# Two gated banded layers on one core: the right projection in four 64x64 tiles instead of two 64x128 tiles with an exchanged second copy

## The chip, the cores and the metric

One NeuronCore of a Trainium2 chip runs the whole program. The metric is the device time of one execution in microseconds, the median of three runs. The engines named below are PE (TensorE, matrix products), PEld (its weight loads), ACT (ScalarE), DVE (VectorE), POOL (GpSimd) and SP (SyncE, which issues most DMAs).

## The reference

Input and output are one 512 x 512 image with 64 channels, float32. Two layers run in sequence, each as x + layer(group_norm(x)). A layer is, with D = 64 and H = 128:

```python
xn = _ln(x, norm_scale, norm_bias)
left = (xn @ Wl + bl) * mask * jax.nn.sigmoid(xn @ Wlg + blg)
right = (xn @ Wr + br) * mask * jax.nn.sigmoid(xn @ Wrg + brg)
out_gate = jax.nn.sigmoid(xn @ Wog + bog)
out = _banded_ingoing(left, right, WIN)
out = _ln(out, out_norm_scale, out_norm_bias) * out_gate
return out @ Wo + bo
```

`_banded_ingoing` mixes along the row axis: row i of the result is the sum, over the nine rows k from i - 4 to i + 4, of left at (k, i) times right at row k, for every column j and every channel on its own. All weights act on 64 or 128 channels, and everything is float32.

## The kernel before

**Tiling.** The 512 rows are cut into nine overlapping blocks of 64 rows, of which 56 (60 at the borders) give output. The two halves of the 512 columns are processed together: partitions 0 to 63 hold the 64 rows of a block at columns j, partitions 64 to 127 the same rows at columns 256 + j. A unit is 8 columns of each half (`JU`), a chunk 8 units; a layer has 36 chunks, and a period of the schedule handles one chunk. So there are 288 units a layer and 576 in all.

**Stages of a unit**, each a step with a name. `load` (SP) fetches the tile z; `scale`, `move` (POOL, some on DVE), `inner` (DVE statistics), `centre`, `resc` (POOL) normalise it. `ztr` transposes it on PE into a bank of PSUM (line 569), `keep0` copies this on ACT into the ring `ZT` (line 583) and `keep1` copies it on ACT a second time, with the two row halves exchanged, into `zT` (line 589). `proj0` and `proj1` are the two halves (4 columns each) of the right projection on PE (`crossed`, line 610): the products with `Wr` and `Wrg` side by side. `sig` is the sigmoid of the gate on ACT (line 630), `right` the product on DVE into `RO` (line 634).

**Stages of a chunk's mixing.** `band` on PE multiplies, per channel, the banded left matrix `A` with `RO` in 64x64 tiles of the array (line 711), `copy` on ACT writes the result back into `RO`. Then, 16 units later, `ost` (statistics), `sa`, `sd` (the norm's factors), `norm0` to `norm7` (ACT, or POOL where the word carries a "!"), `turn0`, `turn1` (transposes on PE, line 844), `gate` (the output gate on PE from `ZT`, line 826), `gated` (its sigmoid on ACT), `tg` (DVE), `last` (the product with `Wo` on PE, line 883), `end` (the residual on DVE), `stp` (the store). Layer 1 also has `sums` on PE (statistics for layer 2's group norm, line 904), layer 2 has `seed` on PE (the bias, line 876).

**Why halves are exchanged.** The band's product of a channel takes row half e of the partitions and writes row half e or its exchange, by the channel's slab s (`e ^ s`, line 723). So for half of the channels (s = 1) `RO` has to hold the two column halves exchanged. `crossed` gets this by taking `ZT` for s = 0 and the exchanged copy `zT` for s = 1 as the stationary operand.

**What sets the order.** Two tables, `FIRST` (line 39) and `SECOND` (line 69), list the steps of a period for layers 1 and 2. A word such as `proj0:2@0` means: half 0 of the projection of the unit 2 places behind the period's first, into PSUM bank pair 0. The loop at line 1117 runs through the table once a period, and each engine executes its instructions in that order. Three bank pairs (`take`, `give`, lines 224 to 235) are shared by `ztr`, `proj`, `gate`, `turn` and `band`; a pair is given back by the step that has read it, for `ztr` this is `keep1`.

The steps of PE in the order of the two tables, each read as a ring, are:

```
FIRST   proj0 proj1 ztr last sums gate band band turn1 turn0 gate proj1 band last turn0 turn1 proj0
        band gate ztr sums last band sums ztr turn1 turn0 proj0 band band gate proj0 turn1 turn0 band
        last ztr gate proj1 last sums turn1 turn0 gate proj1 proj0 ztr sums last turn1 turn0 proj1
        proj0 proj1 ztr sums last sums gate gate turn0 turn1 proj1 proj0 ztr sums last ztr turn0 turn1
        proj0 proj1
SECOND  seed turn1 ztr turn0 last proj0 proj1 band ztr band seed gate proj0 turn0 turn1 band last gate
        turn1 turn0 seed band proj1 ztr last gate proj0 seed ztr turn0 turn1 last proj0 proj1 gate
        proj1 ztr seed turn0 turn1 last ztr proj0 proj1 seed ztr last gate turn0 turn1 proj1 seed
        proj0 proj1 proj0 gate last band turn1 turn0 gate band seed turn0 last ztr turn1 band proj0
        band gate proj1
```

In the profile nearly all instructions carry line 492, that of the helper which keeps the program's order, so they are told apart by the names of their tiles: `banks<-pack,ZT` and `banks<-pack,zT` are the projection, `banks<-RO,A` the band, `banks<-ident,z` and `banks<-ident,on` the transposes `ztr` and `turn`, `banks<-ZT,pack` the gate, `bank<-pack,ZH` is `last`, `acc<-XR` is `sums`, `bank<-pieces,ones` is `seed`. A float32 product on PE makes two records, a transpose one.

Of the kernel before, what the change touches and what calls it, by code (L numbers as in the profile page):

```python
# [31 lines left out]
RING = LAG + 2  # L32
# [8 lines left out]
last:-1 sig1:-1 move:4 sums:-3 scale:10 right0:-1 stp:-2 norm7:0 load:11 keep0:0 ost2:6 gate:0@0  # L41
keep1:0 inner:9 gated:0 right1:-1 band:3@1 norm2:0! norm3:0! move:6 scale:11 move:10 band:2@2
ost3:7 copy:3 turn1:0@0 turn0:0@1 gate:1@1 copy:2 norm0:1 gated:1 inner:7 proj1:0@2 end:-1 norm3:1
tg:0 sig1:0 band:7@0 ost0:4 norm5:1! inner:4 norm1:1! norm7:1 norm4:1! norm6:1! inner:10 norm2:1
last:0 fetch:1 end:0 turn0:1@1 move:11 copy:7 turn1:1@1 proj0:0@0 right1:0 tg:1 norm3:2 sig0:0
resc:2 resc:1 norm4:2 band:0@2 ost1:4 norm1:2 copy:0 right0:0 norm5:2! gate:2@1 ztr:1@0 scale:8
gated:2 norm6:2! sums:-2 last:1 keep0:1 keep1:1 fetch:2 ost0:7 ost2:5 norm2:2! stp:0 inner:6
norm7:2! band:1@2 sums:0 ztr:2@0 copy:1 ost0:5 keep0:2 turn1:2@1 ost1:6 inner:11 norm0:2! load:12
turn0:2@0 inner:5 proj0:1@2 move:8 keep1:2 sa:4 inner:8 norm0:3 scale:12 centre:9 tg:2 sig0:1
band:4@0 sd0:4 norm1:3 end:1 norm3:3! band:6@1 load:13 norm6:3 norm2:3! norm7:3! right0:1 sd1:4  # L50
# [3 lines left out]
norm3:4! ost2:12 norm1:4! sig1:1 last:3 scale:13 norm4:4 scale:14 sums:-1 ost2:15 ost1:13  # L54
turn1:4@2 centre:5 keep1:3 ost3:8 ost3:11 turn0:4@2 gate:5@1 resc:4 gated:5 ost2:10 ost0:11 resc:6
ost1:11 right1:1 tg:4 proj1:2@0 norm5:5! norm7:5! norm4:5! proj0:3@2 ost2:8 ost1:10 norm6:5
ztr:4@1 norm2:5! sig1:2 sig0:3 norm1:5! end:3 centre:8 keep0:4 right1:2 resc:5 right0:3 sums:3
fetch:4 norm3:5 norm0:5 keep1:4 last:4 centre:7 ost3:12 turn1:5@2 load:15 ost0:10 turn0:5@1 end:4
norm6:6 norm7:6! norm1:6 proj1:3@0 centre:10 tg:5 sig1:3 proj0:4@1 sig0:4 stp:-1 proj1:4@2 ost3:10
right1:3 norm4:6! ost1:8 ztr:5@0 norm5:6! sig1:4 fetch:5 right0:4 norm0:6 sums:1 ost0:8 keep0:5  # L60
ost3:9 last:5 sums:2 right1:4 load:16 gate:6@1 resc:7 keep1:5 ost1:9 ost0:9 gate:7@2 ost3:14 sa:8
ost3:13 turn0:6@0 norm2:6! norm3:6! gated:6 gated:7 norm0:7 ost0:14 sd0:8 scale:15 stp:1 fetch:7
move:15 turn1:6@0 sd1:8 norm4:7! norm1:7! centre:11 tg:6 fetch:6 end:5 proj1:5@1 proj0:5@2 sig1:5
ztr:6@0 norm7:7! norm5:7! norm6:7 load:17 sig0:5 norm2:7 right1:5 sums:4 keep0:6 last:6 norm3:7!
move:13 right0:5 ztr:7@2 keep1:6 keep0:7 keep1:7 turn0:7@0 turn1:7@1 sd2:8 proj0:6@1 proj1:6@2
tg:7 stp:3 stp:2 end:6 scale:17 norm5:8! resc:8 load:18 norm4:8 sig0:6 stp:4 fetch:8 sig1:6
# [3 lines left out]
seed:0 inner:8 turn1:1@2 inner:5 ztr:1@0 right1:0 move:11 ost3:5 stp:-1 keep0:1 turn0:1@2 norm5:2!  # L70
last:0 keep1:1 norm0:2 tg:1 inner:10 norm2:2 resc:2 centre:4 norm6:2! proj0:1@1 sa:4 sig0:1
proj1:1@0 norm7:2 end:0 sig1:1 right0:1 band:4@2 copy:4 ztr:2@1 right1:1 band:5@0 centre:5
centre:6 keep0:2 keep1:2 stp:0 sd0:4 norm3:2 seed:1 gate:2@2 inner:11 copy:5! fetch:2 norm4:2
# [4 lines left out]
ost2:9 last:2 ost0:13 ost1:9 fetch:3 end:2 ost3:9 stp:2 keep0:3 sig1:2 right1:2 keep1:3 gate:4@1  # L78
resc:6 proj0:3@2 norm7:4! load:15 seed:3 ost1:15 norm5:4 ztr:4@0 gated:4 centre:10 ost0:9
turn0:4@1 centre:9 sig0:3 ost1:13 load:16 ost0:15 turn1:4@0 right0:3 last:3 keep0:4 keep1:4  # L80
# [4 lines left out]
ost1:10 keep1:5 scale:14 keep0:6 proj0:5@1 move:12 keep1:6 proj1:5@0 ost2:11 norm5:6! fetch:6  # L85
sig0:5 seed:5 stp:3 ztr:7@2 right0:5 fetch:5 last:5 norm7:6 ost2:8 ost2:10 norm2:6! sig1:5
gate:6@1 right1:5 keep0:7 norm6:6! norm0:6 ost2:13 ost0:8 keep1:7 turn0:6@0 scale:15 norm3:6
turn1:6@2 proj1:6@2 fetch:9 gated:6 ost2:12 norm0:7! ost1:8 load:19 sa:8 sig1:6 norm5:7! end:5
# [4 lines left out]
ost1:12 seed:7 resc:8 turn0:8@2 copy:9 last:7 ztr:8@1 gated:8 norm3:8! resc:9 turn1:8@0 norm0:9!  # L93
inner:14 stp:5 ost3:12 norm1:9! inner:12 keep0:8 scale:18 band:14@0 keep1:8 ost2:14 norm5:9 stp:6
tg:8 proj0:8@1 stp:4 ost3:15 norm6:9! norm4:9! ost0:12 band:10@2 norm3:9! fetch:8 fetch:12 norm7:9
# [63 lines left out]
def tile_two_banded_layers(  # L159
# [51 lines left out]
    turns = cycle(range(3))  # L211
# [271 lines left out]
    w = views(pack)  # L483
# [99 lines left out]
    def kept(u: Unit):  # L583
        en.scalar.activation(
            ZT[:, u.at % RING].rearrange("c k (n p) -> c n k p", n=2),
            u.pt.rearrange("c n (k p) -> c n k p", p=S), AF.Identity, bias=1.0,
        )

    def kept_again(u: Unit):
        u.t = ztp.tile([P, JU // 2, P], F32, tag=f"zT{u.at % 2}", name="zT")  # L590
        en.scalar.activation(
            u.t.rearrange("c k (n p) -> c n k p", n=2),
            u.pt.rearrange("c n (k p) -> c n k p", p=S)[:, ::-1], AF.Identity, bias=1.0,
        )
        give(u.bank)
# [14 lines left out]
    def crossed(u: Unit, q: int, w: bass.AP, b: str):  # L610

        u.banks[q], pr = take(b)
        pr = pr.rearrange("p (e k h) -> p e k h", e=2, k=JQ // 2)
        turns = ZT[:, u.at % RING], u.t
        for k in range(JQ // 2):
            for s in range(2):
                for e in range(2):
                    part = slice(e * D, (e + 1) * D)
                    en.tensor.matmul(
                        pr[:, e, k, :].rearrange("p (g s x) -> p g s x", g=2, s=2)[:, :, s],  # L620
                        lhsT=turns[s][part, q // 2 + k],
                        rhs=w[part].rearrange("c (g s x) -> c g s x", g=2, s=2)[:, :, s],
                        start=True, stop=True,
                    )
        return pr
# [290 lines left out]
    def layer(src: bass.AP, dst: bass.AP, w: dict, stats: bool, then=None):  # L916
        per = LH // JC
        n_chunks = len(blocks) * per
        units, outs, lefts, posts = {}, {}, {}, {}
        for c in range(n_chunks):  # L920
            b = blocks[c // per]
            for k in range(NU):
                t = c * NU + k
# [5 lines left out]
        for n in range(n_left):  # L929
            t = n - n_left - 1  # L930
# [77 lines left out]
        def on_keep(n, t, alt, b):  # L1008
            if t in units:
                (kept_again if n else kept)(units[t])  # L1010

# [215 lines left out]
    ZT = keep.tile([P, RING, JU // 2, P], F32, name="ZT")  # L1227
# [19 lines left out]

    ztp = ctx.enter_context(tc.tile_pool(name="ztp", bufs=1))
    wk = ctx.enter_context(tc.tile_pool(name="wk", bufs=3))
# [40 lines left out]
```

## Time and profile before

| | us |
|---|---|
| median of three runs | 4331.73 |
| lowest and highest run | 4329.06, 4340.09 |
| span of the profiled execution, first to last instruction | 4342.3 |

The profiled execution is one of its own; its span is all that the profile has of its time, and it is 10.6 us longer than the median. Layer 1's first transposes start at 229.6 us, behind the statistics of the input and the weights; the last products of layer 2's left operand start at 2358.3 us. The stretch from 600 to 2120 us lies in the midst of layer 1, that from 2700 to 4150 us in the midst of layer 2.

How to read it: a row of groups gives engine, operation, output and inputs, shapes and count, then busy time in us and the mean of one in ns. In PE's rows "64*128" and the like are the rows and columns of the array that the instruction takes, the shape behind it is that of the moving operand. A row of the time order gives start, length from the first start to the last end, and the count of records; ends of PE's records are modelled, so the distance from one row's start to the next row's start tells what a step takes.

### The profile page before, as it was taken

The page shows a single profiled execution, that of the slowest core. Times are in us where ns is not written, and L with a number is a line of the kernel's source. Part 1 is how long each engine was busy: PE and PEld are TensorE (multiplying, and loading weights), DVE is VectorE, ACT ScalarE, POOL GpSimd, SP SyncE. Part 2 cuts the span into 40 slices and gives each one's busy share as a digit, 9 for nine tenths or more (in the row PEclk, how much of TensorE's full clock was granted, in tenths as well). Part 3 has the DMA queues.
Part 4 walks back from the last instruction along what each step waited for, and adds up shares of the span by engine and source line. Part 5 has one row for each costly group of instructions (what it writes and reads, how often), then busy time and mean ns, then how long its engine had stood idle before and what let it go on. Part 6 is the DMA issues. An engine that isn't in the chain of part 4 may idle for free.

```text
span 4342.3 us, 223298 instructions
## 1 busy us (share of the span) xinstructions
PE 3778.1 (87%) x94986; PEld 3263.8 (75%) x94986; DVE 3667.7 (84%) x9911; ACT 3189.2 (73%) x5976; POOL 3754.3 (86%) x4962
## 2 busy tenths in 40 slices
PE   0169899999898999999995889898989899989998
PEld 0058787878787878888874778787878787878786
DVE  8988787878787888888877788898989898989897
ACT  0048787878787877777773778787878787878787
POOL 2379898989898999999956789898989898989894
PEclk9989999999999999999997999999999999999999
DMA  9844545454545454445434344445454545454533
GB/s 393 313 110 108 134 113 143 115 141 114 140 115 138 112 141 120 131 123 129 125 109 114 101 136 124 139 128 138 123 142 122 143 120 145 121 145 121 152 112 100
DMA packets 695719, 596.26 MB, mean 137 GB/s; under 512 B 138310, under 2 KB 549990, under 8 KB 692420
## 3 DMA queue, kind: packets, MB, share of 16 engines
q1 hardware_dynamic: 692212, 580.43, 47.1%
q8 instruction: 748, 12.26, 1.2%
q14 instruction: 247, 2.02, 0.2%
q0 software_dynamic: 2512, 1.56, 0.1%
HBM read 436.71 MB, written 149.74 MB: 135 GB/s over the span
## 4 chain that ended last, share of the span: by engine, by line
PE 46%; POOL 20%; DVE 11%; DMA 9%; SPq 7%; issue 6%; ACT 2%; POOLq 0%; DVEq 0%; ACTq 0%
PE banks L492 35%; POOL z L492 13%; PE bank L492 8%; SPq L492 7%; POOL on L492 6%; PE acc L492 2%; DVE RO L492 2%; DMA z<-in_x_dram 2%; DMA z<-mid_x 2%; DVE gn_st L492 2%; DVE sti L492 1%; DVE sto L492 1%; DVE XR L492 1%; DVE ZH L492 1%; DMA raw<-in_L_conv_Wl_dram 1%
## 5 line engine op out<-in xcount | busy, mean ns | idle before, releaser
L492 POOL TENSOR_SCALAR on<-RO,rs,nm 128x128 f32<-128x128 f32 x2520 | 1129.1, 464 | 157.1 <-PE banks L492 111.2
L492 ACT ACTIVATE on<-RO,nm,rs 128x128 f32<-128x128 f32 x2088 | 971.2, 499 | 106.6 <-PE banks L492 95.2
L492 PE MATMUL banks<-pack,ZT 64*128 64x128 f32 x9216 | 992.3, 287 | 24.1 <-DVE RO L492 13.7
L492 PE MATMUL banks<-pack,zT 64*128 64x128 f32 x9216 | 953.1, 279 | 1.8 <-ACT zT L492 1.0
L492 POOL TENSOR_TENSOR z<-z,ga 128x512 f32<-128x512 f32 x556 | 716.8, 1296 | 261.0 <-DMA z<-mid_x 117.7
L492 ACT ACTIVATE sg<-banks 128x512 f32<-128x512 f32 x1170 | 696.6, 596 | 296.7 <-PE banks L492 270.9
L492 PEld LDWEIGHTS banks<-pack,ZT 64*128 64x128 f32 x9216 | 781.9, 194 | 148.4 <-DVE RO L492 47.5
L492 DVE TENSOR_TENSOR RO<-banks,sg 128x512 f32<-128x512 f32 x1152 | 777.3, 682 | 113.3 <-ACT sg L492 76.6
L492 DVE BATCH_NORM_STATS2 sto<-RO 128x6 f32<-128x256 f32 x2304 | 847.0, 413 | 5.2 <-ACT RO L492 4.0
L492 DVE SCALAR_TENSOR_TENSOR ZH<-banks,pack,ZH 128x896 f32<-128x896 f32 (+1 forms) x576 | 668.0, 1160 | 186.3 <-PE banks L492 155.4
L492 PEld LDWEIGHTS banks<-pack,zT 64*128 64x128 f32 x9216 | 762.2, 194 | 3.5 <-ACT zT L492 2.3
L492 PEld LDWEIGHTS banks<-RO,A 64*64 64x64 f32 x36864 | 617.7, 136 | 159.8 <-DVE RO L492 50.8
L492 PE MATMUL banks<-RO,A 64*64 64x64 f32 x36864 | 694.2, 223 | 48.6 <-issue 20.2
L492 POOL TENSOR_TENSOR z<-z,gb 128x512 f32<-128x512 f32 x556 | 715.7, 1293 | 3.3
L492 ACT COPY RO<-banks 128x1024 f32<-128x1024 f32 x540 | 539.8, 1008 | 194.5 <-PE banks L492 186.4
L492 PE MATMUL bank<-pack,ZH 128*64 128x64 f32 x18432 | 666.2, 226 | 15.7 <-DVE XR L492 5.6
L492 PEld LDWEIGHTS bank<-pack,ZH 128*64 128x64 f32 x18432 | 593.0, 139 | 76.7 <-issue 34.3
L492 ACT ACTIVATE ZH<-banks 128x896 f32<-128x896 f32 (+1 forms) x576 | 531.8, 930 | 142.6 <-PE banks L492 135.2
L492 POOL TENSOR_TENSOR z<-z,rs 128x512 f32<-128x512 f32 x586 | 614.9, 1059 | 19.7 <-DVE rs L492 19.4
L492 POOL TENSOR_TENSOR z<-z,sti 128x512 f32<-128x512 f32 x586 | 620.1, 1072 | 7.6 <-DVE sti L492 7.5
L492 DVE BATCH_NORM_STATS2 sti<-z 128x6 f32<-128x128 f32 x2344 | 505.6, 282 | 120.2 <-POOL z L492 118.0
L492 PE MATMUL banks<-ZT,pack 64*128 64x448 f32 (+1 forms) x2304 | 589.7, 584 | 9.8 <-DVE RO L492 5.5
(202 smaller groups left out, 4169.3 us busy)
## 6 DMA issues: line engine op xcount, KB each, us to landing
z<-in_x_dram SPq DMA_DIRECT2D x576, 128.0 KB
A<-left_of SPq DMA_DIRECT2D x576, 128.0 KB
z<-mid_x SPq DMA_DIRECT2D x576, 128.0 KB
gn_x<-in_x_dram SPq DMA_DIRECT2D x16, 4096.0 KB
XR<-in_x_dram SPq DMA_DIRECT2D x448, 112.0 KB
mid_x<-XR SPq DMA_DIRECT2D x448, 112.0 KB
XR<-mid_x SPq DMA_DIRECT2D x448, 112.0 KB
out_dram<-XR SPq DMA_DIRECT2D x448, 112.0 KB
```

The source lines that it names most:

```text
L492: return lambda *a, **k: tc.keep_in_program_order(f(*a, **k))
```

## The change

The second copy `kept_again` and its steps `keep1` are removed, with the tile pool of `zT`; `kept` gives the bank back. `crossed` takes `ZT` alone. It splits the 128 stationary columns, the two row halves n of a column pair, into two products of 64 columns each, and writes the result of half n to the PSUM partitions of half `n ^ s`. Each product thus takes one of four 64x64 tiles of the array, given by the channel half e (rows) and `n ^ s` (columns). There are 16 products for a half of the projection in place of 8, each with the same 128 moving columns. The tables lose the words `keep1` and are otherwise the same.

```diff
-keep1:0 inner:9 gated:0 right1:-1 band:3@1 norm2:0! norm3:0! move:6 scale:11 move:10 band:2@2
+ inner:9 gated:0 right1:-1 band:3@1 norm2:0! norm3:0! move:6 scale:11 move:10 band:2@2
...
             ZT[:, u.at % RING].rearrange("c k (n p) -> c n k p", n=2),
             u.pt.rearrange("c n (k p) -> c n k p", p=S), AF.Identity, bias=1.0,
         )
-
-    def kept_again(u: Unit):
-        u.t = ztp.tile([P, JU // 2, P], F32, tag=f"zT{u.at % 2}", name="zT")
-        en.scalar.activation(
-            u.t.rearrange("c k (n p) -> c n k p", n=2),
-            u.pt.rearrange("c n (k p) -> c n k p", p=S)[:, ::-1], AF.Identity, bias=1.0,
-        )
         give(u.bank)
...
-        turns = ZT[:, u.at % RING], u.t
+        z = ZT[:, u.at % RING].rearrange("c k (n p) -> c k n p", n=2)
         for k in range(JQ // 2):
             for s in range(2):
-                for e in range(2):
-                    part = slice(e * D, (e + 1) * D)
-                    en.tensor.matmul(
-                        pr[:, e, k, :].rearrange("p (g s x) -> p g s x", g=2, s=2)[:, :, s],
-                        lhsT=turns[s][part, q // 2 + k],
-                        rhs=w[part].rearrange("c (g s x) -> c g s x", g=2, s=2)[:, :, s],
-                        start=True, stop=True,
-                    )
+                for n in range(2):
+                    for e in range(2):
+                        part = slice(e * D, (e + 1) * D)
+                        to = slice((n ^ s) * S, ((n ^ s) + 1) * S)
+                        en.tensor.matmul(
+                            pr[to, e, k, :].rearrange("p (g s x) -> p g s x", g=2, s=2)[:, :, s],
+                            lhsT=z[part, q // 2 + k, n],
+                            rhs=w[part].rearrange("c (g s x) -> c g s x", g=2, s=2)[:, :, s],
+                            start=True, stop=True,
+                        )
         return pr
...
-                (kept_again if n else kept)(units[t])
+                kept(units[t])
...
-    ztp = ctx.enter_context(tc.tile_pool(name="ztp", bufs=1))
```

More of the change, by code (lines that the diff above doesn't have):

```diff
@@ L46 @@
 resc:2 resc:1 norm4:2 band:0@2 ost1:4 norm1:2 copy:0 right0:0 norm5:2! gate:2@1 ztr:1@0 scale:8
-gated:2 norm6:2! sums:-2 last:1 keep0:1 keep1:1 fetch:2 ost0:7 ost2:5 norm2:2! stp:0 inner:6
+gated:2 norm6:2! sums:-2 last:1 keep0:1 fetch:2 ost0:7 ost2:5 norm2:2! stp:0 inner:6
 norm7:2! band:1@2 sums:0 ztr:2@0 copy:1 ost0:5 keep0:2 turn1:2@1 ost1:6 inner:11 norm0:2! load:12
-turn0:2@0 inner:5 proj0:1@2 move:8 keep1:2 sa:4 inner:8 norm0:3 scale:12 centre:9 tg:2 sig0:1
+turn0:2@0 inner:5 proj0:1@2 move:8 sa:4 inner:8 norm0:3 scale:12 centre:9 tg:2 sig0:1
 band:4@0 sd0:4 norm1:3 end:1 norm3:3! band:6@1 load:13 norm6:3 norm2:3! norm7:3! right0:1 sd1:4
@@ L54 @@
 norm3:4! ost2:12 norm1:4! sig1:1 last:3 scale:13 norm4:4 scale:14 sums:-1 ost2:15 ost1:13
-turn1:4@2 centre:5 keep1:3 ost3:8 ost3:11 turn0:4@2 gate:5@1 resc:4 gated:5 ost2:10 ost0:11 resc:6
+turn1:4@2 centre:5 ost3:8 ost3:11 turn0:4@2 gate:5@1 resc:4 gated:5 ost2:10 ost0:11 resc:6
 ost1:11 right1:1 tg:4 proj1:2@0 norm5:5! norm7:5! norm4:5! proj0:3@2 ost2:8 ost1:10 norm6:5
 ztr:4@1 norm2:5! sig1:2 sig0:3 norm1:5! end:3 centre:8 keep0:4 right1:2 resc:5 right0:3 sums:3
-fetch:4 norm3:5 norm0:5 keep1:4 last:4 centre:7 ost3:12 turn1:5@2 load:15 ost0:10 turn0:5@1 end:4
+fetch:4 norm3:5 norm0:5 last:4 centre:7 ost3:12 turn1:5@2 load:15 ost0:10 turn0:5@1 end:4
 norm6:6 norm7:6! norm1:6 proj1:3@0 centre:10 tg:5 sig1:3 proj0:4@1 sig0:4 stp:-1 proj1:4@2 ost3:10
 right1:3 norm4:6! ost1:8 ztr:5@0 norm5:6! sig1:4 fetch:5 right0:4 norm0:6 sums:1 ost0:8 keep0:5
-ost3:9 last:5 sums:2 right1:4 load:16 gate:6@1 resc:7 keep1:5 ost1:9 ost0:9 gate:7@2 ost3:14 sa:8
+ost3:9 last:5 sums:2 right1:4 load:16 gate:6@1 resc:7 ost1:9 ost0:9 gate:7@2 ost3:14 sa:8
 ost3:13 turn0:6@0 norm2:6! norm3:6! gated:6 gated:7 norm0:7 ost0:14 sd0:8 scale:15 stp:1 fetch:7
@@ L64 @@
 ztr:6@0 norm7:7! norm5:7! norm6:7 load:17 sig0:5 norm2:7 right1:5 sums:4 keep0:6 last:6 norm3:7!
-move:13 right0:5 ztr:7@2 keep1:6 keep0:7 keep1:7 turn0:7@0 turn1:7@1 sd2:8 proj0:6@1 proj1:6@2
+move:13 right0:5 ztr:7@2 keep0:7 turn0:7@0 turn1:7@1 sd2:8 proj0:6@1 proj1:6@2
 tg:7 stp:3 stp:2 end:6 scale:17 norm5:8! resc:8 load:18 norm4:8 sig0:6 stp:4 fetch:8 sig1:6
@@ L70 @@
 seed:0 inner:8 turn1:1@2 inner:5 ztr:1@0 right1:0 move:11 ost3:5 stp:-1 keep0:1 turn0:1@2 norm5:2!
-last:0 keep1:1 norm0:2 tg:1 inner:10 norm2:2 resc:2 centre:4 norm6:2! proj0:1@1 sa:4 sig0:1
+last:0 norm0:2 tg:1 inner:10 norm2:2 resc:2 centre:4 norm6:2! proj0:1@1 sa:4 sig0:1
 proj1:1@0 norm7:2 end:0 sig1:1 right0:1 band:4@2 copy:4 ztr:2@1 right1:1 band:5@0 centre:5
-centre:6 keep0:2 keep1:2 stp:0 sd0:4 norm3:2 seed:1 gate:2@2 inner:11 copy:5! fetch:2 norm4:2
+centre:6 keep0:2 stp:0 sd0:4 norm3:2 seed:1 gate:2@2 inner:11 copy:5! fetch:2 norm4:2
 norm1:2! gated:2 centre:3 proj0:2@1 turn0:2@0 turn1:2@2 band:7@2 norm0:3! norm7:3 sd1:4 last:1
@@ L77 @@
 norm1:4! seed:2 band:3@1 norm3:4 norm0:4! copy:3 resc:7 inner:9 proj1:2@0 norm4:4 ost3:8 ztr:3@2
-ost2:9 last:2 ost0:13 ost1:9 fetch:3 end:2 ost3:9 stp:2 keep0:3 sig1:2 right1:2 keep1:3 gate:4@1
+ost2:9 last:2 ost0:13 ost1:9 fetch:3 end:2 ost3:9 stp:2 keep0:3 sig1:2 right1:2 gate:4@1
 resc:6 proj0:3@2 norm7:4! load:15 seed:3 ost1:15 norm5:4 ztr:4@0 gated:4 centre:10 ost0:9
-turn0:4@1 centre:9 sig0:3 ost1:13 load:16 ost0:15 turn1:4@0 right0:3 last:3 keep0:4 keep1:4
+turn0:4@1 centre:9 sig0:3 ost1:13 load:16 ost0:15 turn1:4@0 right0:3 last:3 keep0:4
 norm4:5 tg:4 norm3:5 centre:8 norm1:5! norm6:5 norm7:5! resc:5 load:12 proj0:4@2 ost0:14 sig0:4
@@ L84 @@
 scale:13 ost0:10 right1:4 keep0:5 scale:16 ost3:11 ztr:6@2 scale:12 norm4:6 tg:5 norm1:6! end:4
-ost1:10 keep1:5 scale:14 keep0:6 proj0:5@1 move:12 keep1:6 proj1:5@0 ost2:11 norm5:6! fetch:6
+ost1:10 scale:14 keep0:6 proj0:5@1 move:12 proj1:5@0 ost2:11 norm5:6! fetch:6
 sig0:5 seed:5 stp:3 ztr:7@2 right0:5 fetch:5 last:5 norm7:6 ost2:8 ost2:10 norm2:6! sig1:5
-gate:6@1 right1:5 keep0:7 norm6:6! norm0:6 ost2:13 ost0:8 keep1:7 turn0:6@0 scale:15 norm3:6
+gate:6@1 right1:5 keep0:7 norm6:6! norm0:6 ost2:13 ost0:8 turn0:6@0 scale:15 norm3:6
 turn1:6@2 proj1:6@2 fetch:9 gated:6 ost2:12 norm0:7! ost1:8 load:19 sa:8 sig1:6 norm5:7! end:5
@@ L93 @@
 ost1:12 seed:7 resc:8 turn0:8@2 copy:9 last:7 ztr:8@1 gated:8 norm3:8! resc:9 turn1:8@0 norm0:9!
-inner:14 stp:5 ost3:12 norm1:9! inner:12 keep0:8 scale:18 band:14@0 keep1:8 ost2:14 norm5:9 stp:6
+inner:14 stp:5 ost3:12 norm1:9! inner:12 keep0:8 scale:18 band:14@0 ost2:14 norm5:9 stp:6
 tg:8 proj0:8@1 stp:4 ost3:15 norm6:9! norm4:9! ost0:12 band:10@2 norm3:9! fetch:8 fetch:12 norm7:9
```

## The prediction

> **What bounds the kernel now.** I read the page's busy line and its chain first, then busy time by stretch, then the chain and the waits inside a steady stretch of each layer.
>
> ```profile
> span 4342.3 us, 223298 instructions
> PE 3778.1 (87%) x94986; PEld 3263.8 (75%) x94986; DVE 3667.7 (84%) x9911; ACT 3189.2 (73%) x5976; POOL 3754.3 (86%) x4962
> PE 46%; POOL 20%; DVE 11%; DMA 9%; SPq 7%; issue 6%; ACT 2%; POOLq 0%; DVEq 0%; ACTq 0%
> 600.00:2120.00 1520.00, 1416.28 (x37166) 1240.70 (x37164) 1250.29 (x3349) 1171.98 (x2162) 1421.81 (x1890) 0.98 0.49 128
> 2700.00:4150.00 1450.00, 1354.94 (x33894) 1168.85 (x33892) 1267.09 (x3373) 1198.98 (x2294) 1351.49 (x1727) 0.97 0.48 133
> by line: PE banks L492 42.3%; POOL z L492 12.0%; PE bank L492 9.3%; issue 5.9%; POOL on L492 5.5%; PE acc L492 4.7%; DMA z<-in_x_dram 4.6%; SPq L492 4.3%; DVE RO L492 1.9%; DMA mid_x<-XR 1.3%; DVE sti L492 1.3%; DVE ZH L492 1.2%; DVE XR L49
> by line: PE banks L492 31.1%; POOL z L492 17.6%; SPq L492 10.5%; POOL on L492 9.7%; PE bank L492 7.6%; issue 7.2%; DMA z<-mid_x 4.1%; DVE RO L492 2.4%; DMA out_dram<-XR 1.7%; DVE sto L492 1.3%; DVE XR L492 1.2%; DVE sti L492 1.0%; DVE rsqrt
> ```
>
> The stretch rows give length, then busy time of PE, PEld, DVE, ACT and POOL. In layer 1 (600 to 2120 us) PE and POOL are both busy for 93% and ACT for 77%; in layer 2 (2700 to 4150 us) 93%, 93% and 83%. The two chain lines are for the same stretches: PE's three names make 42.3 + 9.3 + 4.7 = 56.3% of the chain in layer 1 and 31.1 + 7.6 = 38.7% in layer 2, POOL and DMA most of the rest. ACT holds 2% of the whole chain. So of PE's busy time, 56.3 / 93.2 = 0.60 lies on the path in layer 1 and 38.7 / 93.4 = 0.41 in layer 2. **The change takes work from ACT, which hardly sets the end, and rearranges PE, which does.**
>
> The waits of PE in the two stretches say the same (who waited for whom, us, times, longest); the last two rows, of ACT's groups, are what the change removes and what it keeps:
>
> ```profile
> PE banks L492 <- POOL on L492: 33.9, 27, 4.6
> PE banks L492 <- POOL z L492: 31.7, 12, 4.0
> ...
> PE banks L492 <- POOL on L492: 70.9, 34, 5.3
> ...
> PE banks L492 <- ACT on L492: 0.4, 2, 0.2
> ...
> L492 ACT ACTIVATE zT<-banks 128x512 f32<-128x512 f32 x576 | 344.0, 597 | 0.0
> L492 ACT ACTIVATE ZT<-banks 128x512 f32<-128x512 f32 x576 | 342.4, 595 | 110.8 <-PE banks L492 107.2
> ```
>
> **ACT's part.** Removed: 576 zT copies of 597 ns, 344.0 us of busy time. PE waits 0.4 us for ACT in layer 2's stretch and ACT is 2% of the chain, so what lies under these copies is ACT's own slack. If the 2% (87 us) shrank as zT's share of ACT's work (344.0 / 3189.2 = 11%), the gain were 9 us; the least is nothing. I take -5. The bank of the transposes is also given back one copy earlier, and the projection no longer waits for the second copy; by the wait rows neither is short.
>
> **PE's part: the streams.** A half of the projection was 16 records in 64x128 tiles (two tiles at once), and becomes 32 records in 64x64 tiles (four at once), of the same 128 columns. The engine's order of time in two stretches (start, length, count) has all rows that are needed:
>
> ```profile
> 1006.81 2.15 PE L492 MATMUL banks<-RO,A 64*64 64x64 f32 x128
> 1008.89 0.71 PE L492 MATMUL banks<-ident,on 64*128 64x64 f32 x16
> 1009.44 0.97 PE L492 MATMUL banks<-ZT,pack 64*128 64x448 f32 x4
> ...
> 1021.07 0.66 PE L492 MATMUL banks<-ident,on 64*128 64x64 f32 x16
> 1021.57 0.44 PE L492 MATMUL banks<-pack,ZT 64*128 64x128 f32 x4
> 1021.85 0.39 PE L492 MATMUL banks<-pack,zT 64*128 64x128 f32 x4
> ...
> 3127.72 0.92 PE L492 MATMUL banks<-ZT,pack 64*128 64x448 f32 x4
> 3128.47 0.46 PE L492 MATMUL banks<-pack,ZT 64*128 64x128 f32 x4
> ...
> 3150.83 1.19 PE L492 MATMUL banks<-RO,A 64*64 64x64 f32 x64
> 3151.95 0.49 PE L492 MATMUL banks<-pack,ZT 64*128 64x128 f32 x4
> 3152.27 0.39 PE L492 MATMUL banks<-pack,zT 64*128 64x128 f32 x4
> 3152.50 0.39 PE L492 MATMUL banks<-pack,ZT 64*128 64x128 f32 x4
> 3152.72 0.39 PE L492 MATMUL banks<-pack,zT 64*128 64x128 f32 x4
> 3153.04 1.19 PE L492 MATMUL banks<-RO,A 64*64 64x64 f32 x64
> 3154.16 1.02 PE L492 MATMUL banks<-ZT,pack 64*128 64x448 f32 x4
> 3155.02 0.39 PE L492 MATMUL banks<-pack,ZT 64*128 64x128 f32 x4
> ```
>
> Four projection records start every 0.223 us, two at a time, so a wave of two takes 111.6 ns and a half 8 waves, 0.893 us. The band's product already runs in four 64x64 tiles: 128 records take 2.08 us to the next start (1006.81 to 1008.89), 64 take 1.12 (3150.83 to 3151.95), so 64 records are 0.96 us, a wave of four with 64 columns 60 ns. For four tiles with 128 columns the bounds are 111.6 (no dearer than two tiles) and twice 60, 120 ns. I take 113.3, the old wave plus a few ns for the two further tiles, nearer the row with the same columns. Eight waves cost 0.906 us: 0.0136 more a half, 0.22 us in a period of 16 halves. Twice the instructions do the same work in the same time.
>
> **PE's part: the switches.** The 64x128 projection stood among transposes and gates that also use 64x128 tiles. From its last start at 3152.72 to the band's first it is 0.32 us where the rhythm is 0.22: leaving 64x128 tiles costs 0.10. A band run of 64 records takes 1.12 where the streams take 0.96: first weights and leaving together 0.16. The first four projection records behind the band take 0.32 (3151.95 to 3152.27), again 0.10 for first weights of 128 columns. Sixteen transposes take 0.55 behind the band (1008.89) and 0.50 without a switch (1021.07): 0.05. A gate takes 0.86 behind the band (3154.16) and 0.75 behind the projection (3127.72): 0.11. I give 64-column weights 0.05, half of 128's, which leaves 0.11 for leaving 64x64 tiles. So a switch costs **0.15 us into the new projection, 0.16 out of it to transposes, 0.22 out of it to a gate**. A projection behind transposes pays 0.06 already (1021.57 to 1021.85 is 0.28).
>
> Now the order of the steps (the lists of PE's steps, read as rings). FIRST has 4 gate to projection (+0.60), 5 turn to projection (0.09 each, +0.45), 4 projection to ztr and 1 to turn (+0.80), 3 projection to band (no switch any more, 0.15 each, -0.45), 1 projection to last (+0.01): **+1.41 us a period**. SECOND has 4 gate to projection (+0.60), 3 projection to turn or ztr (+0.48), 4 projection to seed (0.16 as for transposes, +0.64), 2 projection to gate (+0.44), one each from ztr, turn and seed (+0.33), 2 projection to band (-0.30), 2 band to projection (0.21 each, -0.42), 2 last to projection (0.05 each, -0.10): **+1.67 us**. With the streams 1.63 and 1.89 us; 36 periods each, 59 + 68 = 127 us more of PE.
>
> The Trainium skill, TensorEngine Tiling (Array Packing), section Key Properties, says that a change of the tiling mode, not just of the tile, drains the engine. By the 0.32 against 0.22 us the trace agrees; the page gives no figure. If only the streams counted, the sum were 0.22 us a period, 16 us of PE.
>
> **On the path.** If the path stays where it is, it grows by 0.60 x 59 + 0.41 x 68 = 63 us, and a longer path of the same links can't end earlier. If PE sets everything, it is 127. PE now waits 1520 - 1416 = 104 us in 28.8 periods of 52.7 us (the chain of that stretch repeats in that time), 3.6 a period, and 2.0 would be left; POOL is as busy. I take the lower end and a third of the rest: 63 + 21 = 84.
>
> ```profile
> 1025.52 3.53 PE banks L492 x100
> ...
> 1078.22 3.53 PE banks L492 x100
> ...
> L492 PE MATMUL banks<-RO,A 64*64 64x64 f32 x36864 | 694.2, 223 | 48.6 <-issue 20.2 <-DVE RO L492 16.2 <-DVE rsqrt_u L492 8.7
> L492 PEld LDWEIGHTS banks<-RO,A 64*64 64x64 f32 x36864 | 617.7, 136 | 159.8 <-DVE RO L492 50.8 <-issue 29.6 <-ACT RO L492 26.2
> ```
>
> The band's records wait 20.2 us for "issue", that is for nothing that the profile shows, most likely for instructions: they use theirs up fastest. 18,432 further pairs on 94,986 are 19% more; I add 6 us (from 0 to twice the 20.2). Sum: 84 + 6 - 5 = **+85 us** on the profiled 4342.3, so 4427; that execution lies 10.6 above the median of 4331.73, and I predict **4417 us**. Prices of 0.15 us read from rows rounded to 0.01 are good to 7%, 9 us of the 127. So the case's own range is 4377 (63 - 9 for ACT at its most - 9) to 4474 (127 + 6 + 9).
>
> **Rivals.**
>
> 1. *A tile waits for its weights.* The new order uses tiles as AABB CCDD CCDD AABB, (row half, column half) of (0,0), (1,0), (0,1), (1,1), where a record pair is one product. The next A has to be loaded past two C and two D that wait. If the engine can't, each of four alternations a half shows a first weight load, 0.05 us: 0.20 x 1152 = 230 us on PE, half of it on the path, 4417 + 115 = 4532 (4450 to 4600). For it: the band goes round its tiles evenly, and nothing in this trace has two pairs in a row. Against it: in the band too, records of one tile follow each other in pairs and four tiles still run at once.
>
> 2. *PE's waits swallow it.* The 3.6 us of waits a period exceed the 1.63; if they are free on the path, the time stays at 4332, or at 4340 with half of the streams' 16 us on the path (4320 to 4372, where at most a third of the switches counts). Against it: more than half of layer 1's chain is PE itself.
>
> 3. *Faster: ACT's queue was the hidden limit.* Each zT delays the sigmoid, norm or copy behind it by about 0.5 us (3151.06 to 3151.54 below), DVE's products wait for sigmoids, and banks come free with them. DVE waits 76.6 us for ACT's sg in all; if half of that lies on the path and the switches fall into PE's waits, 4332 - 38 + 8 = 4302. It decides if more of ACT's delays than of PE's switches reach the path; 2% against 46% of the chain speak against it.
>
> ```profile
> 3151.06 0.59 ACT L492 ACTIVATE zT<-banks 128x512 f32<-128x512 f32 x1
> 3151.54 0.89 ACT L492 ACTIVATE on<-RO,nm,rs 128x128 f32<-128x128 f32 x2
> ...
> L492 DVE TENSOR_TENSOR RO<-banks,sg 128x512 f32<-128x512 f32 x1152 | 777.3, 682 | 113.3 <-ACT sg L492 76.6
> ```
>
> 4. *Weights never load beside a product of the same rows.* Then each of 8 waves a half would show its whole load, 136 ns by the band's weight row: 1.09 us x 1152, less PE's waits, some 5400 us. The band's 60 ns waves with loads of 136 ns refute it. The Trainium skill, TensorE: Matmul & The Clock Gate, section The mechanism, says that loads overlap only with products of another row group; here the trace says otherwise, and the trace decides.
>
> That the change doesn't do what it says is not likely: the band shows that the four tiles run at once.
>
> **Numbers.** Chances: my forecast 0.70; rival 1 0.12; rival 2 0.12 (of it 0.07 within 0.3%, 0.05 slower); rival 3 0.05; rival 4 0.01. Slower by over 0.3% (13 us, about what a measurement of this kernel can tell from no change): 0.70 + 0.12 + 0.05 + 0.01 = 0.88; within 0.07; faster 0.05. The range takes in the forecast's own, the lower half of rival 1's (where the bound of 120 ns for a wave lies too) and the top of rival 2's: 4355 to 4520.
>
> **What would show it.** Right: ACT's busy time falls by some 340 us with no end moved; a half of the projection takes about 0.91 us from first to last start in an even rhythm; 0.15 us stands between a gate or transposes and the projection, and nothing between it and the band; PE's share of the chain rises and its waits for POOL shrink. Wrong: gaps of 0.05 us inside a half (rival 1), a PE that waits for POOL as long as before (rival 2), or sigmoids that come earlier with DVE's products behind them (rival 3). A first start of the projection behind a gate in the plain rhythm would take the switches out of the sum.

## The result and the profile after

| | before, us | changed, us |
|---|---|---|
| median (lowest to highest) | 4331.73 (4328.07 to 4346.16), 5 runs | 4438.66 (4417.79 to 4440.58), 5 runs |
| span of the profiled execution | 4342.3 | 4415.6 |

The ratio is 1.0228, with a 95% interval of 1.0207 to 1.0250: 107 us slower. Forecast were 4417 us and 85 us more, in a range of 4355 to 4520. The profiled execution of the changed kernel is its fastest of five, and its span is only 73 us longer than that of the kernel before, so its trace shows the loss at its smallest.

The page after: span, busy times with instructions, PE's instruction queue (packets, MB, share), the chain by engine, and PE's groups of the projection and of the band.

```profile
span 4415.6 us, 259199 instructions
PE 3839.3 (87%) x113418; PEld 3175.8 (72%) x113418; DVE 3683.1 (83%) x9911; ACT 2938.3 (67%) x5400; POOL 3748.7 (85%) x4962
q8 instruction: 891, 14.60, 1.4%
PE 61%; DVE 11%; POOL 9%; DMA 7%; SPq 6%; issue 5%; ACT 2%; DVEq 0%; POOLq 0%; ACTq 0%
L492 PE MATMUL banks<-pack,ZT 64*64 64x128 f32 x36864 | 1221.1, 278 | 38.1 <-DVE RO L492 18.7
L492 PE MATMUL banks<-RO,A 64*64 64x64 f32 x36864 | 703.3, 222 | 67.5 <-issue 54.0
```

ACT lost 251 us of busy time (3189.2 to 2938.3), less than the 340 forecast. The prediction took the sum of the copies' records, 344.0 us, but these overlap their neighbours: the copy shown there lasts 0.59 us and the next record starts after 0.48. The busy line counts an overlap once. PE's share of the chain rose from 46% to 61%, and POOL's fell from 20% to 9%. Two rows point at something that the forecast had priced at almost nothing: the band waits 54.0 us for "issue" where it was 20.2, and the program comes in 891 packets. Before, the same queue had 748:

```profile
q8 instruction: 748, 12.26, 1.2%
```

PE's waits in the two stretches of before (600 to 2120 and 2700 to 4150 us), changed kernel:

```profile
PE banks L492 <- POOL on L492: 35.1, 21, 6.3
PE banks L492 <- POOL z L492: 32.8, 13, 4.7
PE banks L492 <- issue: 32.2, 49, 1.9
...
PE banks L492 <- POOL on L492: 55.9, 16, 4.9
PE banks L492 <- issue: 17.6, 29, 1.4
```

and the two rows of "issue" in the kernel before:

```profile
PE banks L492 <- issue: 17.2, 24, 2.0
...
PE banks L492 <- issue: 5.6, 11, 1.0
```

The waits for POOL are about what they were in layer 1 and fell by 15 us in layer 2 (70.9 to 55.9). Those for instructions went from 17.2 to 32.2 and from 5.6 to 17.6 us. PE's order of time in the changed kernel (start, length, count, and idle time before the row) shows both the switches and these waits:

```profile
1022.05 0.97 PE L492 MATMUL banks<-ZT,pack 64*128 64x448 f32 x4
1022.96 1.10 PE L492 MATMUL banks<-pack,ZT 64*64 64x128 f32 x32
1023.88 1.14 PE L492 MATMUL banks<-RO,A 64*64 64x64 f32 x64
...
1026.67 1.10 PE L492 MATMUL banks<-pack,ZT 64*64 64x128 f32 x32
1027.59 0.78 PE L492 MATMUL banks<-RO,A 64*64 64x64 f32 x37
1028.57 0.70 PE L492 MATMUL banks<-RO,A 64*64 64x64 f32 x27 [0.20 <-issue]
...
1035.02 1.10 PE L492 MATMUL banks<-pack,ZT 64*64 64x128 f32 x32
1035.94 0.66 PE L492 MATMUL banks<-RO,A 64*64 64x64 f32 x32
1036.83 1.67 PE L492 MATMUL banks<-RO,A 64*64 64x64 f32 x96 [0.23 <-issue]
...
3011.25 1.98 PE L492 MATMUL banks<-pack,ZT 64*64 64x128 f32 x64
3013.15 1.02 PE L492 MATMUL banks<-ZT,pack 64*128 64x448 f32 x4
3014.11 1.10 PE L492 MATMUL banks<-pack,ZT 64*64 64x128 f32 x32
3015.14 0.46 PE L492 MATMUL banks<-ident,z 64*128 64x64 f32 x8
...
3036.24 1.19 PE L492 MATMUL banks<-RO,A 64*64 64x64 f32 x64
3037.25 1.05 PE L492 MATMUL banks<-pack,ZT 64*64 64x128 f32 x32
3038.13 1.14 PE L492 MATMUL banks<-RO,A 64*64 64x64 f32 x64
```

From start to start, a half of the projection between two bands takes 0.88 us (3037.25 to 3038.13), no more than the 0.893 of the old one. Between a gate and transposes it takes 1.03 (3014.11 to 3015.14), and the gate that stands between two projections 0.96 (3013.15 to 3014.11). Twice here the band, right behind a projection, stops in the middle with "issue" as its only reason: after 37 of its 64 records, and after 32 of 128.

To follow PE through whole executions I summed, over the trace's records of PE from 300 us on, the distances from each start to the next. Idle gaps of over 30 ns are taken out and stand in columns of their own, by what ended them. The last column counts changes between tile modes from 255 us on, in program order.

| kernel | PE's own steps, us | waits for other engines | waits for "issue" (times) | mode switches |
|---|---|---|---|---|
| before | 3707 | 296 | 35 (67) | 2012 |
| changed | 3767 | 272 | 72 (140) | 2820 |

The 808 further switches are 11.2 a period on average; the lists of steps give 11 more in layer 1 and 12 more in layer 2. Beside the waits for instructions, which doubled, PE's own steps grew by 60 us, where 127 were forecast, and the waits for other engines fell by 24.

### The profile page after: what moved, and what is told of

The parts are those of the page before. It is cut to its first block, busy times and chain, and to the rows that moved or that the text cites. A ratio compares the mean times of both kernels' runs of the same rounds, so it can differ in the third digit from the quotient of the medians.

```text
span 4415.6 us, 259199 instructions
## 1 busy us (share of the span) xinstructions
PE 3839.3 (87%) x113418; PEld 3175.8 (72%) x113418; DVE 3683.1 (83%) x9911; ACT 2938.3 (67%) x5400; POOL 3748.7 (85%) x4962
## 3 DMA queue, kind: packets, MB, share of 16 engines
q8 instruction: 891, 14.60, 1.4%
## 4 chain that ended last, share of the span: by engine, by line
PE 61%; DVE 11%; POOL 9%; DMA 7%; SPq 6%; issue 5%; ACT 2%; DVEq 0%; POOLq 0%; ACTq 0%
PE banks L492 47%; PE bank L492 11%; SPq L492 6%; POOL z L492 6%; PE acc L492 3%; POOL on L492 3%; DVE RO L492 2%; DVE gn_st L492 2%; DMA z<-in_x_dram 2%; DVE sti L492 1%; DVE sto L492 1%; DVE XR L492 1%; DMA z<-mid_x 1%; DVE ZH L492 1%; DVE z L492 1%
## 5 line engine op out<-in xcount | busy, mean ns | idle before, releaser
L492 PE MATMUL banks<-pack,ZT 64*64 64x128 f32 x36864 | 1221.1, 278 | 38.1 <-DVE RO L492 18.7
L492 PEld LDWEIGHTS banks<-pack,ZT 64*64 64x64 f32 x36864 | 1037.2, 136 | 266.2 <-DVE RO L492 71.2
L492 PE MATMUL banks<-RO,A 64*64 64x64 f32 x36864 | 703.3, 222 | 67.5 <-issue 54.0
L492 PEld LDWEIGHTS banks<-RO,A 64*64 64x64 f32 x36864 | 638.7, 136 | 159.2 <-issue 69.5
L492 PE MATMUL banks<-ident,on 64*128 64x64 f32 x9216 | 467.4, 230 | 120.2 <-POOL on L492 111.3
L492 PEld LDWEIGHTS banks<-ident,on 64*128 64x128 f32 x9216 | 389.4, 140 | 216.6 <-POOL on L492 140.0
```

What stands on the lines that cost most here:

```text
L492: return lambda *a, **k: tc.keep_in_program_order(f(*a, **k))
```

## The experiments

The theory after the result was that switches and instructions together cost the time. The rivals were that ACT's relief hides part of a larger loss, that the tiles' order stalls PE, and, later, that the exchange itself is dear. Every run has the kernel before timed on the same chip beside it, and each ratio is to that.

### The second copy put back

In the kernel before, only `crossed` is replaced by the new one, so that ACT still makes the copy that nobody reads.

```diff
+        z = ZT[:, u.at % RING].rearrange("c k (n p) -> c k n p", n=2)
...
+                        to = slice((n ^ s) * S, ((n ^ s) + 1) * S)
+                        en.tensor.matmul(
+                            pr[to, e, k, :].rearrange("p (g s x) -> p g s x", g=2, s=2)[:, :, s],
+                            lhsT=z[part, q // 2 + k, n],
```

> The changed projection on PE, but with ACT's second, exchanged copy still made (nobody reads it): the change without its relief of ACT. Theory (ACT lies off the path, PE's added time is the whole effect): like the changed kernel, 4425 to 4450 us. Rival (the relief of ACT gave back some of PE's cost): slower than the changed kernel by what the relief is worth, 4460 us or more if that is over 20 us.

Measured: 4466.33 us against 4346.55, a ratio of 1.0282 (1.0265 to 1.0299). That lies above the 4425 to 4450 us expected, where the rival had put it. But the kernel before was 15 us slower on this chip, and the changed kernel had not been timed beside this one, so it was run again (below).

### ACT's relief alone

The old 64x128 tiles with no second copy; both slabs take `ZT`, so the exchange is left out. Against the kernel before, beside the removal of the copy:

```diff
-        turns = ZT[:, u.at % RING], u.t
+        turns = ZT[:, u.at % RING], ZT[:, u.at % RING]
```

> The old projection in 64x128 tiles, without the second copy; both slabs read the first copy, so the exchange of the row halves is left out. ACT's relief without PE's cost. Theory: 5 to 10 us faster than before at most, 4320 to 4332. Rival (ACT's queue was a hidden limit): about 4300 or less.

Measured: 4343.28 us against 4346.55, a ratio of 0.9993 (0.9977 to 1.0009). The busy row of its page:

```profile
PE 3767.5 (87%) x94986; PEld 3257.7 (75%) x94986; DVE 3667.7 (85%) x9911; ACT 2934.0 (68%) x5400; POOL 3755.4 (87%) x4962
```

ACT loses its 255 us here as well, and the time does not move by anything that the interval can tell from none. So ACT's queue was not the hidden limit (rival 3). The copy put back, at 1.0282 (1.0265 to 1.0299), can't be told from the changed kernel's own repeats (below, 1.0270 and 1.0256, with intervals that overlap its own). Neither run shows a part of ACT in the loss.

### The tiles in even turn

The changed kernel with its products in the tile order A B C D A B C D (AABB CCDD AABB CCDD in records); the exchange moves to the choice of the stationary half.

```diff
-                        to = slice((n ^ s) * S, ((n ^ s) + 1) * S)
+                        to = slice(n * S, (n + 1) * S)
...
-                            lhsT=z[part, q // 2 + k, n],
+                            lhsT=z[part, q // 2 + k, n ^ s],
```

> The changed kernel with the two column halves in the same order for both slabs, so that the tiles follow as AABB CCDD AABB CCDD and none gets two products in a row. Theory (the streams run evenly already): the changed kernel's time within 0.5%, and a half of the projection between two bands at 0.87 us as there. Rival (a tile waits for its weights): faster by 50 us or more.

Measured: 4468.71 us, a ratio of 1.0279 (1.0250 to 1.0307). An even order gains nothing: the ratio is no lower than the changed kernel's, and a half between two bands takes a median of 0.873 us in both. So rival 1 falls. Its order of time holds a further sign, though:

```profile
1044.15 1.14 PE L492 MATMUL banks<-RO,A 64*64 64x64 f32 x64
1045.22 1.02 PE L492 MATMUL banks<-ZT,pack 64*128 64x448 f32 x4
...
1048.06 1.54 PE L492 MATMUL banks<-RO,A 64*64 64x64 f32 x64
1049.53 0.69 PE L492 MATMUL acc<-XR 120*64 120x65 f32 x16
```

The first band run of 64 records reaches the next start in 1.07 us, the second in 1.47, and no wait is marked on it, since this view marks none under 150 ns. Inside the second run one record starts 0.335 us behind the last, and the trace has only 0.117 of that as idle. Ends of PE's records are modelled, so a pause within a group can be drawn as work. The column "waits for issue" is a lower bound, and the rest is in "PE's own steps".

### A dose of switches

The kernel before with one 64x64 product of 64 columns ahead of the projection's first half, in every second unit, and then in every unit. The product that follows overwrites its result.

```diff
+        if q == 0 and u.at % 2 == 0:
+            en.tensor.matmul(
+                pr[:S, 0, 0, :S], lhsT=turns[0][:D, 0, :S], rhs=w[:D, :S], start=True, stop=True
+            )
```

> The kernel before with one small 64x64 product put ahead of every second unit's first half (its result is overwritten): 4 more stays in 64x64 tiles a period, about 0.10 + 0.05 on the way in and 0.11 + 0.10 on the way out, so some 1.4 us a period or 104 us on PE, with the streams, ACT and the number of instructions as before. Theory (switches reach the end): 4395 to 4435 us. Rival (PE's waits swallow switches, and the loss of the change comes from the doubled instructions): under 4360.

> The small 64x64 product ahead of every unit's first half: twice the dose, about 930 switches more than before (the change brought 808), with the number of instructions nearly as before. Theory (each switch reaches the end at the same rate as in the first dose, 38 us for 466): 76 us, a ratio of 1.017. If PE's slack is used up by the first dose, 1.020 or more. Rival (switches hardly count, the first dose was the products themselves): under 1.012.

| | time, us | ratio (95%) | switches added | PE's own steps | waits for others | "issue" |
|---|---|---|---|---|---|---|
| every second unit | 4382.74 | 1.0087 (1.0070 to 1.0103) | 466 | 3785 (+78) | 273 | 23 |
| every unit | 4453.59 | 1.0248 (1.0234 to 1.0262) | 1008 | 3876 (+169) | 247 | 26 |

My forecast for the first dose, 4395 to 4435, was too high. The second came out above the 1.017 of a steady rate, as expected for a PE whose slack is used up. The first dose costs 36 us (4382.74 - 4346.55), 0.08 us a switch and 0.46 of what it adds to PE's steps. The double dose costs 107 us (4453.59 - 4346.52), 0.11 us a switch and 0.63 of the added steps. **A first helping of PE work is half swallowed by PE's waits, and the next one less.** Yet the changed kernel, with 60 to 80 us added to its steps (the table above and the last one below) against the first dose's 78, lost three times as much. So by what they add to PE's steps, switches alone can't be its cause. By their number they still could be most of it: 808 at 0.08 to 0.11 us are 65 to 89 us. The kernel with half the records, below, decides that.

### The changed kernel again, and more records in the old tiles

`more_records` is the kernel before with each projection product cut in two of 64 moving columns. It has as many records as the changed kernel, in the old 64x128 tiles and with the old switches.

```diff
+                    for g in range(2):
+                        en.tensor.matmul(
+                            pr[:, e, k, :].rearrange("p (g s x) -> p g s x", g=2, s=2)[:, g, s],
+                            lhsT=turns[s][part, q // 2 + k],
+                            rhs=w[part].rearrange("c (g s x) -> c g s x", g=2, s=2)[:, g, s],
```

> The changed kernel itself, unaltered, beside the other runs of this call, because the copies of it with ACT's second copy or with other tiles came out at 1.028 of the kernel before and it at 1.023. Theory (PE waits for its instructions, and how long differs from run to run): between 1.020 and 1.030, with more time in PE's waits for nothing that the profile shows where it is slower. Rival (ACT's relief is worth 20 us): 1.023 again.

> The kernel before with every product of the right projection cut into two of 64 moving columns, still in 64x128 tiles: as many PE instructions as the changed kernel, and not one more switch. Its streams cost more (32 records at the transposes' pace of 31 ns, 0.99 us a half against 0.89, some 115 us on PE). Theory (PE runs out of instructions): PE's waits for nothing shown rise from 35 us to over 60, as in the changed kernel, and the time to 4420 to 4480. Rival (these waits belong to the 64x64 tiles): they stay near 35 and the time stays below 4420.

The changed kernel again: 4456.55 us against 4346.52, a ratio of 1.0270 (1.0253 to 1.0287). `more_records`: 5209.73 us, a ratio of 1.1993 (1.1976 to 1.2009). That was far outside what I had expected, and PE's waits for "issue" fell to 14 us (31 times), where the theory had over 60 and its rival 35. Its order of time and its page say why.

```profile
1206.10 0.66 PE L492 MATMUL banks<-pack,ZT 64*128 64x64 f32 x8
1206.54 0.66 PE L492 MATMUL banks<-pack,zT 64*128 64x64 f32 x8
```

```profile
q8 instruction: 892, 14.61, 1.2%
L492 PE MATMUL banks<-RO,A 64*64 64x64 f32 x36864 | 688.7, 223 | 13.8 <-issue 8.3
```

Eight records take 0.446 us on average, 55.8 ns each, as before with twice the columns. The projection's time doubles, and the test no longer asks its question. It answers another one: as many instructions as in the changed kernel (14.61 MB against 14.60) and yet the band waits 8.3 us for "issue" in place of 54.0. **The number of instructions alone did not starve PE here; they have to be used up fast as well.**

### Half the records in the new tiles

So the new 64x64 tiles and the new switches were kept, and the records halved: one product of 256 moving columns in place of two of 128. The exchange can't be had this way and is left out.

```diff
-            for s in range(2):
-                for n in range(2):
-                    for e in range(2):
...
+            for n in range(2):
+                for e in range(2):
+                    part = slice(e * D, (e + 1) * D)
+                    to = slice(n * S, (n + 1) * S)
+                    en.tensor.matmul(
+                        pr[to, e, k, :], lhsT=z[part, q // 2 + k, n], rhs=w[part],
```

> The changed projection with the two slabs in one product of 256 moving columns, which leaves out the exchange of the row halves: 64x64 tiles, switches and total columns as in the changed kernel, but 16 records a half in place of 32, as many PE instructions as before. Theory (part of the loss is that PE runs out of instructions): PE's waits for nothing shown fall to 35 us or less, a half still takes about 0.87 us, and the time falls by 30 to 60 us to a ratio of 1.012 to 1.020, which is what the switches alone cost. Rival (the instructions' number does not matter): 1.027 as the changed kernel.

> The changed kernel unaltered, for the comparison on the same chip: 1.023 to 1.028.

Measured: 4366.12 us against 4348.23, a ratio of 1.0035 (1.0023 to 1.0047), and the changed kernel on the same chip 4461.95, a ratio of 1.0256 (1.0232 to 1.0281). Almost all of the loss is gone, 96 us where 30 to 60 were expected. This kernel makes all 808 further switches, and together with its streams and ACT's relief they cost 18 us, not the 65 to 89 that the doses suggest. But this kernel also leaves out the exchange, so a last pair cuts that apart: the changed kernel without the exchange and with all its records, beside the same kernel with half of them. The two compute the same.

```diff
-                        to = slice((n ^ s) * S, ((n ^ s) + 1) * S)
+                        to = slice(n * S, (n + 1) * S)
```

> The changed kernel with each product's result left in its own row half (the exchange is left out), still 32 records of 128 columns a half of the projection. It does the same work as half_the_records (16 records of 256 columns), in the same tiles with the same switches; only the count of records differs. Theory (the doubled instructions cost the time): 4440 to 4480 us, ratio about 1.026 as for the changed kernel, and PE's waits for issue at 70 to 105 us. Rival (the exchange itself, or the side that a result goes to, costs what half_the_records saved): about 4366 us, ratio 1.003.

> half_the_records unaltered (the exchange is left out), on the same chip as no_exchange_full_records, so that the two differ in nothing but the cut of the products. Both theories: about 4366 us, ratio 1.003, PE's waits for issue near 40 us.

| | time, us | ratio (95%) | PE's own steps | waits for others | "issue" (times) |
|---|---|---|---|---|---|
| all records | 4457.00 | 1.0276 (1.0259 to 1.0293) | 3772 | 274 | 82 (148) |
| half the records | 4362.94 | 1.0053 (1.0038 to 1.0068) | 3736 | 290 | 30 (59) |
| `half_the_records`, the first time | 4366.12 | 1.0035 (1.0023 to 1.0047) | 3738 | 282 | 39 (65) |
| changed kernel, beside `half_the_records` | 4461.95 | 1.0256 (1.0232 to 1.0281) | 3780 | 274 | 85 (162) |
| changed kernel again | 4456.55 | 1.0270 (1.0253 to 1.0287) | 3787 | 269 | 91 (161) |

Without the exchange but with all records the loss is whole (1.0276 against 1.0256 and 1.0270 with it), so no cost of the exchange shows. The records cost 94 us (4457.00 - 4362.94). Twice the records are also twice the weight loads, but these hardly lengthen a half: 0.873 us against 0.863 between two bands. In the two profiled executions (spans 4434.1 and 4360.8, 73 us apart) PE's own steps take 36 us more, the waits for "issue" 52 more, and the waits for other engines 16 less: 72 in all, of the 73. First the band, then PE's waits in layer 1's stretch, with all records:

```profile
L492 PE MATMUL banks<-RO,A 64*64 64x64 f32 x36864 | 702.4, 222 | 76.3 <-issue 61.0 <-DVE RO L492 6.9 <-ACT RO L492 1.7
```

```profile
PE banks L492 <- issue: 37.7, 56, 1.9
PE banks L492 <- POOL z L492: 31.0, 12, 4.2
PE banks L492 <- POOL on L492: 29.1, 24, 5.8
```

and with half of them:

```profile
L492 PE MATMUL banks<-RO,A 64*64 64x64 f32 x36864 | 687.7, 222 | 40.3 <-issue 22.4 <-DVE RO L492 9.7 <-DMA A<-left_of 1.9
```

```profile
PE banks L492 <- POOL on L492: 41.6, 31, 5.9
PE banks L492 <- POOL z L492: 34.6, 16, 4.2
PE banks L492 <- issue: 8.2, 14, 1.1
```

The order of these rows is the finding: in this stretch PE waits most for POOL with half the records, as before, and most for its own program with all of them. In layer 2 POOL stays ahead in both.

### What "issue" is here

The queue named "instruction" with 748 and 891 packets is PE's program, by its size. The changed kernel has 18,432 records more, each with a weight load, so 36,864 instructions, and 143 packets more of 16,384 bytes: 63.6 bytes an instruction, so about 257 instructions a packet, or 128 pairs of load and product. The Trainium skill, Perfetto Trace Analysis, section The 4-stage abstract model, gives an instruction 64 bytes; the 63.6 agree, and a packet would hold 256.

The trace can test this. I numbered PE's loads, products and semaphore instructions in the order of the program. Of the 140 waits for "issue" in the changed kernel, 139 stand at one and the same place of every 256, at a load or its product; in the kernel before it is 65 of 67, with half the records 59 of 59. So PE waits where one packet ends and the next begins, and hardly anywhere else. The late record in the 1.47 us band run above stands at this place too.

The same place shows the pauses that are drawn as work. For each record I took the distance from the start before it, without the idle time counted as waits, and compared it with the median of the same pair of steps. At this place of 256 the excess stands far above the mean of the other 127 pairs of places, whose standard deviation is under 2 us:

| kernel | marked waits at the place, us | excess not marked, us |
|---|---|---|
| before | 35 | 18 |
| changed | 72 | 34 |
| all records, no exchange | 82 | 34 |
| half the records | 30 | 13 |
| `more_records` | 14 | 11 |

In the trace's list of packets from 300 us on, the next one never starts much earlier than 3.4 us behind the last: the shortest 1% of intervals are below 3.39 us before and 3.36 after, the median is 4.74 and 4.16. Of the 140 waits, 139 also end between 1.1 and 1.65 us behind the landing of such a packet; of PE's records at large 12% start in such a place. In the kernel before it is 65 of 67. So **the wait is one for the next 128 pairs, and the closest that packets came is 3.4 us / 128 = 26.6 ns a pair**. That this is a limit is argued from the shortest intervals, which are alike in all the kernels; no run tests it. The packets that PE waited for came no closer than others (a median of 4.16 us behind the last), and nine in ten of the waits end 2.2 to 2.9 us behind the start of the packet, so the delay of a single packet counts too. Against this stands what PE uses:

| group | ns a pair | from |
|---|---|---|
| band | 15 | 0.96 us for 64, in the prediction |
| old projection | 55.8 | 0.223 us for 4, there too |
| new projection | 27.5 | 0.88 us for 32 |
| projection with half the records | 54 | 0.863 us for 16, the median from start to start between two bands in that trace |

The band always uses pairs faster than they were ever seen to come. The old projection uses them at half that rate, so most likely a reserve stands ready for the band behind each one. The new projection uses them about as fast as they come, so the reserve isn't filled, and the band behind it stops after 32 or 37 records, as the order of time shows. The place of the waits is measured; the reserve is an inference. `more_records` fits: as many pairs as in the changed kernel, at 55.8 ns in the projection, and waits of 14 us in all.

## Why the prediction was right, and where it was not

The direction came out, and the measured 107 us against 85 lies in the range. That the sum came so near is luck: two of its terms are wrong and offset each other. The cost was put on the switches, and most of it was a wait for instructions.

**ACT's part (-5 us).** Right within what can be measured: relief alone gives 0.9993 (0.9977 to 1.0009), 3 us of 4346.

**The streams (0.893 to 0.906 us a half).** The size was small, as forecast, but the sign was wrong: 0.88 us between two bands. Four tiles at once with 128 columns are no dearer here than two.

**The prices of a switch.** Right in the rows read here. A gate between two projections takes 0.96 where a gate behind the projection took 0.75: 0.21, from 0.11 at its front and 0.10 at its back. A projection between 64x128 neighbours takes 1.03 where it takes 0.88 between bands: 0.15, from 0.05 in and 0.11 out by the forecast. The first start behind a gate is not in the plain rhythm, and nothing stands between the projection and the band, as forecast.

**127 us more of PE.** Mis-sized. The kernel with half the records has all 808 switches, the new tiles and ACT's relief, and PE's steps grew by 29 us (3736 - 3707). The streams account for part of what is missing: 0.893 to 0.863 us in 1152 halves are 35 us less, and forecast were 16 more. Of the 98 us missing they explain 51. ACT's relief alone has 11 us less of PE's steps in its trace (3696), but 7 of these are pauses between packets (12 not marked, against 18 before), which differ from run to run. The other 47 us stay open.

**On the path (84 us).** Too large, for the same reason. Switches, streams and relief together cost 18 us in one run (4366.12 - 4348.23) and 24 in the other (4362.94 - 4338.84). Of the 29 us added to PE's steps 0.62 to 0.83 reached the end, though steps and times come from different executions; the forecast had 84 / 127 = 0.66, and the two doses 0.46 and 0.63. So the share was about right, and the size of the steps wrong.

**"Issue" (+6, at most twice the 20.2 us).** This is the step that failed. I scaled the present waits by the count of pairs, 19% more, and wrote that twice the instructions do the same work in the same time. Inside a projection they do. But the program has to come in as well, and the new projection went from 55.8 to 27.5 ns a pair, about as fast as packets were seen to come. Doubling the records cost 94 and 96 us in two pairs on two chips (4457.00 - 4362.94; 4461.95 - 4366.12). In the profiled executions of the first pair, 73 us apart, the waits marked between packets are 52 us more (82 - 30) and the pauses not marked there 21 more (34 - 13). The streams add 1152 x (0.873 - 0.863) = 12 us, by the medians between two bands in the two kinds of kernel, and the waits for other engines fall by 16, so that the two nearly cancel. The second pair has 46 us (85 - 39) and 22 (36 - 14) at the same place, where the spans are 81 us apart. The medians of the first pair stand 21 us further apart than its spans, since its profiled execution with all records is the fastest of four; no trace shows that part. The spread of the changed kernel speaks for it as well: five profiled kernels with these tiles, records and exchange (the changed one, its two repeats, the copy put back, the tiles in turn) have waits for "issue" of 72, 85, 91, 97 and 104 us and spans of 4415.6, 4445.6, 4450.9, 4460.3 and 4468.7 us, more than a microsecond of span for each one of waits, though in runs whose medians of the kernel before differ by up to 17 us.

So the parts as measured are 18 to 24 for what I had put at 79 (84 - 5), and 94 to 96 for what I had put at 6. They are not strictly additive: by the two doses of switches, about half of the first work added to PE was free and less of what followed. Had the records come alone, they might have cost less.

**The rivals.** A tile that waits for its weights (1): refuted by the 0.88 us and by the even order, which gains nothing. PE's waits swallow it (2): half true for the switches, wrong for the whole. ACT's hidden limit (3): refuted by relief alone. Loads never beside products of the same rows (4): refuted, since four tiles on two row halves take 0.88 us for 8 waves, 110 ns each, less than one load of 136.

No version here beats the kernel before. Even half the records without the exchange stand at 1.0035 and 1.0053, and relief alone can't be told from 1.

## What to carry to other kernels

Before a product is cut into more and shorter ones, work out the nanoseconds per pair of load and product over the next 128 pairs or so, and not only the time on the array: the program has to arrive at that rate, and here the group that follows with the fastest rhythm paid. A wait for "issue" that is small in the trace of before is no bound on the risk: 35 us became 72 to 91 in the changed kernel. And the removed copy, on an engine that holds 2% of the chain, bought nothing to set against that.

## What the runs showed of the hardware

- **PE's program arrives while it runs, and PE can wait for it.** Packets of 16,384 bytes, 128 pairs, follow each other at 3.3 us or more (26 ns a pair) before and after, and 139 of 140 waits for "issue" stand where a packet begins. In layer 1's stretch of 1520 us the changed kernel has these (the view of DMA queues: packets, MB, share):

```profile
q8 instruction: 338, 5.54, 1.5%
```

  That is one in 4.5 us on average, further apart than the closest. PE stops 140 times in the whole execution all the same, most likely since its groups use the pairs unevenly.
- **In 64x128 tiles the moving columns can be free.** Records of 64 columns in `more_records` follow each other at 55.8 ns, as those of 128 columns do. Something else sets the pace there. In 64x64 tiles it doesn't: a wave takes 60 ns with 64 columns and 110 with 128. The nearest suspect is the load. Its row in the kernel before (mean 194 ns) stands against 136 ns for a 64x64 load, but no run has cut it apart:

```profile
L492 PEld LDWEIGHTS banks<-pack,ZT 64*128 64x128 f32 x9216 | 781.9, 194 | 148.4 <-DVE RO L492 47.5
```

- **Four tiles cost no more than two.** A wave of 128 moving columns takes 110 ns with four 64x64 tiles and 111.6 with two 64x128 tiles.
